# A mixture-of-experts block: the choice of experts for the second image computed in two parts, the Gelu table loaded earlier, one store on another queue

## The chip, the cores and the metric

The kernel runs on one core of a Trainium2 chip. The metric is device time in microseconds (us) of one execution, as a median over runs. The core has TensorE (matmuls, "PE" in the profile), VectorE ("DVE"), ScalarE ("ACT"), GpSimd ("POOL") and SyncE ("SP"), each working through its own list of instructions in order, with semaphores between them. SP, ACT and POOL also have a list of DMA transfers each.

## The reference, cut to what matters

Two images (batches) of 256 channels and 56 x 56 = 3136 pixels go through three stages. The first is a linear form of attention with a convolution-like mixing of channels. Its result, as 3136 tokens of 256 channels, goes through causal attention with four heads and then through a layer of eight experts, of which each token uses the two with the largest probabilities:

```python
t = _to_tokens(x)
t = t + _L1_attn_ref(_ln_t(t), L1_attn_W_attn, L1_attn_W_proj)
t = t + _L1_ffn_ref(_ln_t(t), L1_ffn_gate_w, ...)

# in _L1_ffn_ref
logits = xf @ gate_w + gate_b
probs = jax.nn.softmax(logits, axis=-1)
top2_vals, top2_idx = jax.lax.top_k(probs, 2)
cw = jnp.zeros((N, Ee)).at[jnp.arange(N)[:, None], top2_idx].add(top2_vals)
# per expert: out += cw[:, e] * (gelu(xf @ w1 + b1) @ w2 + b2)
```

All arithmetic is in 32-bit floats.

## The kernel before, in words

**Tiles.** A batch of 3136 tokens is 25 tiles of 128 rows, the last of 64 (`NCH = 25`). A tile of `ts[b]` holds the token's 256 channels, its 8 logits, and columns for mean, variance (later the inverse deviation, `RSTD`) and slot.

**Attention** (`attend`, L708 on) runs for batch 0 and then batch 1. Queries go in 7 blocks of 448 (`NB`), and for each block two pairs of heads (`hp`). One such block and pair is called a visit here. A visit goes through the key tiles up to the diagonal in steps; the last block has 25 steps a visit. A step issues the scores' matmul (L745), their Exp on ScalarE (L753), a mask on VectorE where the tile touches the diagonal (L755), the addition to the sums of exponentials on VectorE (L767), and, three steps late, the product with the values (L785). Two steps after a visit's end its sums go through a matmul (`sp`, L809), a copy, two trips through DRAM and a reciprocal; `later` holds what is due: `invert` (L829) four steps on, `scale` (L841) six after that, `hand_on`, which only counts the block as finished, two after that.

**The queue.** Everything else is written as generators, kept in `queue`. `pull(n)` gives `n` turns: it goes through the queue from the front, and the first generator that yields True has used one turn; one that yields False is passed over. Every step of attention calls `pull()` once (in `between`). So a generator nearer the front takes all turns that it can use. `tokens(b)` is the main generator of a batch: `project_out` (matmul L683, addition L688) for every tile whose block is finished, with a `closer` for its mean and variance (L177, L178, one turn a tile), and then `dispatch`.

**`dispatch(b)`** (L1028 on) begins when every tile of the batch is closed (`unclosed[b] == 0`). It is the choice of experts: an inverse square root by four Newton iterations on 128 x 25 values (L1062 to L1081), logits, softmax (Exp on ScalarE, L1098), and twice a maximum and its place (L1118 to L1130), on 128 x 25 x 8 values, up to `both`, the 0/1 table of the two chosen experts (L1136, L1139). Then come two matmuls, `rank` (L1150) and `total` (L1152), for each token's place among the tokens of its expert, the slots' arithmetic, and the distribution: each tile is normalised (L1383) and two indirect DMAs on POOL put its rows at their slots in DRAM (`x_slots`, L1391). Batch 0 does this while batch 1's attention runs, one operation per turn (`op`). Batch 1's attention is the last, so its choice runs beside the experts' work, in pieces of three to five operations per turn (`small_piece`). `one_hot` (L1254 on) makes the experts' numbers and biases of the blocks, with a matmul `bp`.

**The experts.** `experts` goes through blocks of 128 slots, one a pass (`n` from -1 on): `hidden` (matmul `ht`, L1512, then four Gelu activations, L1521), the transposes of block n + 2 (`tp`, L1489, copied by ScalarE, `xT`, L1493), the weights of a block copied by VectorE (`w`, L1500), and `outputs` of block n - 3 (`yp`, L1531, with the bias added by VectorE, L1541). Blocks up to 42 (`FULL0`) hold tokens of batch 0 alone, so these passes can run before batch 1 is chosen; the rows of blocks from 42 on are fetched in pass 36, and `need(1)` sees to it that the distribution of batch 1 is finished by then. At the end of every pass `meanwhile` counts `turn` and pulls: 4 turns while batch 1 is projected and not sent, 2 or 3 while it is being distributed, 2 otherwise.

**`closing`** is first in the queue after attention. It carries out what is left in `later` for the last visit, at set passes: `invert` after three turns, `scale` after three more, and `hand_on` in the same pass as `scale`.

**The order on each engine** is the order in which this program issues instructions (the scheduling is by hand), so a matmul from `dispatch` stands in TensorE's list behind the pass in whose `meanwhile` it was issued.

**The end.** The last columns of batch 1 are two halves of a PSUM result, copied by ScalarE and by VectorE and stored by `store_last(0)` and `store_last(1)` (L1638 to L1642), both through ScalarE's queue, with the rest of the queue's work (`settle`) between them.

Of the kernel before, what the change touches and what calls it, by code (L numbers as in the profile page):

```python
# [10 lines left out]
F32 = mybir.dt.float32  # L11
U32 = mybir.dt.uint32
I32 = mybir.dt.int32
# [15 lines left out]
def conv_attn_moe_kernel(  # L29
# [99 lines left out]
    def chunk(j):  # L129
        return min(P, N - j * P)  # L130
# [381 lines left out]
    def layer1(nm, general):  # L512

        with ExitStack() as whole:
# [361 lines left out]
            def attend_general(b, qT, kT, v):  # L876
# [5 lines left out]
                with ExitStack() as inner:  # L882
# [139 lines left out]
                    for n in range(len(order)):  # L1022
# [2 lines left out]
                        values(state)  # L1025
                        state = ahead

            def dispatch(b):  # L1028

                t = ts[b]  # L1030
                tail = chunk(NCH - 1)

                def small_piece():

# [13 lines left out]
                def small(name, last=E, dt=F32):  # L1048
                    return g1.tile([P, NCH, last], dt, tag=name, name=f"{name}_{nm}{b}")

                def wide(ap):
                    return ap.to_broadcast([P, NCH, E])

                pr = small("lg")
                red = small("red", 1)


                var = t[:, :, RSTD]
                x, y, z = (
                    small(k, 1).rearrange("p t o -> p (t o)") for k in ("newton_x", "newton_y", "red")  # L1060
                )
                nc.vector.tensor_scalar(x, var, 1e-5, None, ALU.add)  # L1062
                yield from op()
                nc.vector.tensor_scalar(
                    y.bitcast(I32), x.bitcast(I32), 1, None, ALU.arith_shift_right
                )
                yield from op()
                nc.vector.tensor_scalar(
                    y.bitcast(I32), y.bitcast(I32), -1.0, float(0x5F3759DF), ALU.mult, ALU.add
                )  # L1070
                yield from op()
                yield from small_piece()
                for i in range(4):
                    to = var if i == 3 else y
                    nc.vector.tensor_tensor(z, y, y, ALU.mult)
                    yield from op()
                    nc.vector.tensor_tensor(z, z, x, ALU.mult)
                    yield from op()
                    nc.vector.tensor_scalar(z, z, -0.5, 1.5, ALU.mult, ALU.add)
                    yield from op()  # L1080
                    nc.vector.tensor_tensor(to, y, z, ALU.mult)  # L1081
                    yield from op()
                    yield from small_piece()
                nc.vector.tensor_tensor(
                    pr, t[:, :, C : C + E], wide(t[:, :, RSTD : RSTD + 1]), ALU.mult
                )
                yield from op()
                nc.vector.tensor_tensor(
                    pr, pr, gb.unsqueeze(1).to_broadcast([P, NCH, E]), ALU.add
                )  # L1090
                yield from op()
                nc.vector.tensor_reduce(red, pr, AX.X, ALU.max)
                yield from op()
                nc.vector.tensor_tensor(pr, pr, wide(red), ALU.subtract)
                yield from op()
                yield from small_piece()
                yield from apart(3)
                nc.scalar.activation(pr, pr, AF.Exp)  # L1098
                yield from small_piece()
                yield from apart(3)  # L1100
                nc.vector.tensor_reduce(red, pr, AX.X, ALU.add)
                yield from op()
                nc.vector.reciprocal(red, red)
                yield from op()
                nc.vector.tensor_tensor(pr, pr, wide(red), ALU.mult)
                yield from op()
                yield from small_piece()


                ids = rev.unsqueeze(1).to_broadcast([P, NCH, E])  # L1110
                at = small("at")
                left = small("left")
                picks = []
                src = pr
                for k in range(2):
                    top = wts[b][:, :, k : k + 1]
                    one = small(f"one{k}")
                    nc.vector.tensor_reduce(top, src, AX.X, ALU.max)  # L1118
                    yield from op()
                    nc.vector.tensor_tensor(at, src, wide(top), ALU.is_equal)  # L1120
                    yield from op()
                    nc.vector.tensor_tensor(at, at, ids, ALU.mult)
                    yield from op()
                    yield from small_piece()
                    nc.vector.tensor_reduce(red, at, AX.X, ALU.max)
                    yield from op()
                    nc.vector.tensor_tensor(one, at, wide(red), ALU.is_equal)
                    yield from op()
                    if k == 0:
                        nc.vector.scalar_tensor_tensor(left, one, -2.0, pr, ALU.mult, ALU.add)  # L1130
                        yield from op()
                        src = left
                    picks.append(one)
                    yield from small_piece()
                both = small("both")
                nc.vector.tensor_tensor(both, picks[0], picks[1], ALU.add)  # L1136
                yield from op()
                if tail < P:
                    nc.vector.memset(both[tail:, NCH - 1], 0.0)  # L1139
                    yield from op()  # L1140
                flat = both.rearrange("p t e -> p (t e)")
                yield from small_piece()

                if b:
                    yield True
                for _ in range(0 if b else 2):
                    yield True

                rank = bank(f"rank_{b}")
# [104 lines left out]
                def one_hot(eb, w):  # L1254

                    nc.vector.tensor_copy(eblks[b], eb[:, :w])
                    hot = g1.tile([E, w], F32, tag="hot", name=f"hot_{nm}{b}")
                    nc.vector.tensor_tensor(hot, eb[:E, :w], row.to_broadcast([E, w]), ALU.is_equal)
                    yield from small_piece()
                    for _ in range(1 if b else 4):  # L1260
                        yield True
                    bp = bank(f"bp_{b}", (P, KH, w))
                    for k in range(KH):
                        nc.tensor.matmul(bp[:, k, :], b1s[:, k, :], hot, start=True, stop=True)
                    nc.vector.tensor_copy(b1bs[b], bp)
                    ranked[b] = True
                    yield from small_piece()
# [139 lines left out]
            def experts(w1s, w2s, b2s, ex, es, ps6, between, need, written, settle, decide):  # L1407
# [230 lines left out]
                def store_last(o):  # L1638

                    ot = hots[o]  # L1640
                    (nc.vector.tensor_copy if o else nc.scalar.copy)(ot, sums_of[o][:, :REST])
                    nc.scalar.dma_start(out=out[B - 1, o * P : (o + 1) * P, LAST * P :], in_=ot)  # L1642

                direct, tail, sums_of = {}, [], []

# [302 lines left out]
            if general:  # L1948
                centre_gate(bank)
                fold_gate(bank, turn_gate(bank))  # L1950
                for b in range(B):
                    xs, qks, vs = project_qkv(b, qT, kT, v, px)
                    for piece in xs(0) + [p for s in range(NS) for p in qks(s) + vs(s) + xs(s + 1)]:
                        piece()
                    attend_general(b, qT, kT, v)
                    queue.append(tokens(b, qT, lambda: N))
                    while not projected[b]:
                        pull(every=True)
            else:
# [43 lines left out]
                    piece()  # L2003
                for b in range(B):
                    batches.append(tokens(b, qT, lambda b=b: min(finished[b])))
                    queue.append(batches[b])

                    def visit(i, hp):

                        now, then = ahead(b, i, hp)  # L2010
                        ring.append(0)
                        for piece in now:
                            piece()
                        for _ in range(2):
                            products()
                        for piece in then:
                            piece()
                        ring.clear()
# [18 lines left out]
            def closing():  # L2037

                if not general:

                    while finished[B - 1][NH - 1] < N:
                        until = turn[0] + (3 if later[0][0] - clock[0] > 2 else 0)
                        while turn[0] < until:
                            yield False
                        clock[0] = max(clock[0], later[0][0])
                        due(clock[0])
# [8 lines left out]
            with ExitStack() as moe:  # L2055
# [37 lines left out]
                def meanwhile():  # L2093
                    gathered[0] = stored[0] = 0
                    turn[0] += 1
                    if placed[1] and not sent[1]:
                        pull(2 if turn[0] % 3 else 3, every=True)
                    else:
                        pull(
                            4 if worked[0] >= MIXED or projected[1] and not sent[1] else 2, every=True  # L2100
                        )
                    if side and next(side[0], None) is None:
                        side.popleft()
# [188 lines left out]
```

## Time and profile before

| | us |
|---|---|
| median of 3 runs | 1283.17 (1280.9 to 1288.38) |
| the profiled execution | 1271.12 |
| its span | 1269.3 |
| TensorE busy | 1247.0 |
| VectorE busy | 783.7 |
| ScalarE busy | 614.4 |
| GpSimd busy | 360.5 |

The span reaches from the first to the last instruction of the profiled execution. In it the convolution stage reaches to about 93 us, attention to 848, the experts from 849 to 1253, and the rest is the end. A line of the trace gives the start, the length, the engine, the source line, the operation with its output and inputs, the number of instructions and, in brackets, how long the engine stood idle before and what it was waiting for. A line of the waits gives the total, the number and the longest.

### The profile page before, as it was taken

What the parts mean: (1) busy time and instruction counts of PE and PEld (TensorE: products, weight loads), DVE (VectorE), ACT (ScalarE), POOL (GpSimd) and SP (SyncE); (2) the same over time, 40 slices, a digit from 0 to 9 for tenths busy, and PEclk for the clock granted to TensorE, in tenths of its full rate; (3) what the DMA queues carried; (4) which work ended last, traced back from release to release, by engine and by line L of the source; (5) the groups of instructions that cost most, each with busy time, mean ns of one, the idle gap of its engine ahead of it and who ended that gap; (6) DMA issues with size and microseconds to landing.
All of it is one profiled execution on the core that took longest, in us unless ns stands there. A gap on an engine that the chain in (4) does not pass through costs nothing.

```text
span 1269.3 us, 28520 instructions
## 1 busy us (share of the span) xinstructions
PE 1247.0 (98%) x10809; PEld 815.8 (64%) x10809; DVE 783.7 (62%) x1673; ACT 614.4 (48%) x1235; POOL 360.5 (28%) x319
## 2 busy tenths in 40 slices
PE   8999999999999999999999999999899999999997
PEld 8875545444444444545445444458899999999996
DVE  2583567676777754567676888764854443465563
ACT  0255555565656556455464656553333333344442
POOL 1103231110002204231111666200076212676650
PEclk9999999999999999999999999999999999999999
DMA  9995101000000000100000223542154433466653
GB/s 319 359 346 176 24 18 33 26 9 25 9 18 9 25 2 9 42 10 16 9 10 17 67 69 107 196 129 71 57 162 143 130 112 99 147 208 201 210 166 121
DMA packets 111073, 123.87 MB, mean 98 GB/s; under 512 B 19703, under 2 KB 100840, under 8 KB 110930
## 3 DMA queue, kind: packets, MB, share of 16 engines
q1 hardware_dynamic: 100130, 95.18, 24.6%
q0 software_dynamic: 9840, 25.67, 6.1%
q8 instruction: 89, 1.46, 0.5%
q10 hardware_dynamic: 960, 1.11, 0.3%
q14 instruction: 54, 0.44, 0.1%
HBM read 62.06 MB, written 61.05 MB: 97 GB/s over the span
## 4 chain that ended last, share of the span: by engine, by line
PE 95%; DVE 2%; ACT 1%; issue 0%; DMA 0%; DVEq 0%; ACTq 0%
PE yp_f L785 21%; PE sc_f L745 20%; PE ht_f L1512 14%; PE yp_f L1531 13%; PE qk_f L614 7%; PE v_f L629 4%; PE pp_f L683 3%; PE cp L410 3%; PE gram L317 2%; PE tp_f L1489 2%; PE sp_f L809 1%; PE yo_f L1758 1%; PE xp_f L600 1%; DVE acc_f L767 1%; PE tail_f L1623 0%
## 5 line engine op out<-in xcount | busy, mean ns | idle before, releaser
L767 DVE TENSOR_TENSOR acc_f<-acc_f,st_f 128x896 f32<-128x896 f32 (+5 forms) x372 | 373.0, 1003 | 127.2 <-ACT st_f L753 117.1
L753 ACT ACTIVATE st_f<-sc_f 128x896 f32<-128x896 f32 (+5 forms) x400 | 330.6, 838 | 202.4 <-PE sc_f L745 181.1
L785 PE MATMUL yp_f<-st_f,v_f 64*64 64x448 f32 (+6 forms) x3184 | 337.2, 500 | 2.7 <-DVE st_f L755 1.5
L745 PE MATMUL sc_f<-qT_f,kT_f 64*64 64x448 f32 (+6 forms) x3184 | 335.8, 498 | 1.2 <-ACT st_f L753 1.1
L1521 ACT ACTIVATE g_f<-ht_f,b1b 128x128 f32<-128x128 f32 x408 | 116.7, 369 | 218.0 <-PE ht_f L1512 217.9
L745 PEld LDWEIGHTS sc_f<-qT_f,kT_f 64*64 64x64 f32 x3184 | 119.0, 133 | 153.9 <-issue 140.4
L785 PEld LDWEIGHTS yp_f<-st_f,v_f 64*64 64x64 f32 x3184 | 116.7, 133 | 155.0 <-issue 127.5
L1512 PE MATMUL ht_f<-xT_f,w_f 128*128 128x128 f32 x1632 | 200.3, 276 | 1.4 <-ACT xT_f L1493 1.4
L1512 PEld LDWEIGHTS ht_f<-xT_f,w_f 128*128 128x128 f32 x1632 | 197.0, 192 | 6.4 <-ACT xT_f L1493 1.8
L797 POOL TENSOR_TENSOR qT_f<-acc_f 128x448 f32<-128x448 f32 x28 | 32.0, 1144 | 455.0 <-ACT acc_f L796 455.0
L1391 POOL DMA_INDIRECT x_slots<-xr_f,idx x100 | 120.7, 1207 | 140.1 <-DVE edge_f L1303 67.1
L585 POOL TENSOR_SCALAR xn_f<-t 128x256 f32<-128x256 f32 (+1 forms) x50 | 85.0, 1708 | 157.8 <-PE xp_f L600 68.6
L1500 DVE COPY w_f<-w1s_f 128x1024 f32 x102 | 72.1, 708 | 68.1 <-PE ht_f L1512 66.5
L1541 DVE TENSOR_TENSOR ys_f<-yp_f,kT_f 128x128 f32<-128x128 f32 x102 | 29.6, 290 | 102.9 <-PE yp_f L1531 102.7
L1552 POOL DMA_INDIRECT y_tokens<-ys_f,to_f x57 | 58.8, 1031 | 116.1 <-DVE ys_f L1541 94.2
L614 PE MATMUL qk_f<-px_f,wat 128*128 128x512 f32 (+2 forms) x224 | 88.2, 546 | 0.6 <-ACT px_f L606 0.6
L614 PEld LDWEIGHTS qk_f<-px_f,wat 128*128 128x128 f32 x224 | 40.6, 190 | 45.7 <-issue 41.0
L1709 POOL DMA_INDIRECT y_f<-y_slots,idx x50 | 57.2, 1144 | 17.2 <-issue 16.9
L755 DVE TENSOR_TENSOR st_f<-st_f,keep 128x256 f32<-128x256 f32 (+1 forms) x112 | 44.9, 401 | 26.9 <-ACT st_f L753 26.5
L1531 PE MATMUL yp_f<-px_f,g_f 128*128 x204 | 60.9, 380 | 0.0
L1531 PE MATMUL yp_f<-v_f,g_f 128*128 x204 | 60.7, 379 | 0.0
L1531 PE MATMUL yp_f<-kT_f,g_f 128*128 x204 | 60.7, 379 | 0.0
(285 smaller groups left out, 1224.0 us busy)
## 6 DMA issues: line engine op xcount, KB each, us to landing
x_slots<-fill SPq DMA_DIRECT2D x1, 8190.0 KB
xb_f<-x_slots SPq DMA_DIRECT2D x60, 130.0 KB
x_slots<-fill SPq DMA_DIRECT2D x1, 7296.0 KB
y_slots<-ys_f SPq DMA_DIRECT2D x57, 128.0 KB
kept<-t SPq DMA_DIRECT2D x2, 3200.0 KB
x<-in_x_dram SPq DMA_DIRECT2D x14, 448.0 KB
rb_f<-inverses SPq DMA_DIRECT2D x56, 112.0 KB
y_f<-y_tokens SPq DMA_DIRECT2D x23, 256.0 KB
```

Source lines behind the costliest of these rows:

```text
L585: nc.gpsimd.tensor_scalar(xn[:k, a], ts[b][:k, n + a, :C], ts[b][:k, n + a, MEAN : MEAN + 1], ts[b][:k, n + a, RSTD : RSTD + 1], ALU.subtr ...
L614: nc.tensor.matmul(ps[:, :w], wat[:, c, d0 : d0 + P], px[:, s % 2, c, :w], start=(c == 0), stop=(c == NH - 1),)
L745: nc.tensor.matmul(ps[h : h + HS, a, c0:W], kT[hp][rows, j * P + h : j * P + h + HS], qT[rows, hp, q0 + c0 : q0 + W], start=True, stop=True,)
L753: nc.scalar.activation(st[:k, :, c0:], ps[:k, :, c0:W], AF.Exp, scale=SCALE)
L767: nc.vector.tensor_tensor(acc[:k, :, c0:], acc[:k, :, c0:], st[:k, :, c0:], ALU.add)
L785: nc.tensor.matmul(yp[a * HS : (a + 1) * HS, h // HS, c0:W], v[hp][h : h + HS, j, a, :HS], st[h : h + HS, a, c0:], start=first, stop=bool( ...
L1391: s = nc.gpsimd.indirect_dma_start(out=xds[b], out_offset=bass.IndirectOffsetOnAxis(ap=idxs[b][:kk, k, n : n + 1], axis=0), in_=xr[:kk], i ...
L1500: nc.vector.tensor_copy(w, w1s[:, :, bass.ds(e, 1), :].rearrange("p c e h -> p c (e h)"))
L1512: nc.tensor.matmul(ht[:, k, :], w[:, c, k * P : (k + 1) * P], xT[:, c, :], start=(c == 0), stop=(c == NH - 1),)
L1521: nc.scalar.activation(g[:, k, :], ht[:, k, :], AF.Gelu, bias=b1bs[b][:, k, i : i + 1])
L1531: nc.tensor.matmul(yp[:, :C], g[:, k, :], w2s[k][:, bass.ds(e, 1), :].rearrange("p e d -> p (e d)"), start=(k == 0), stop=(k == KH - 1),)
L1552: s = nc.gpsimd.indirect_dma_start(out=y_tokens, out_offset=bass.IndirectOffsetOnAxis(ap=to[:, n % GB : n % GB + 1], axis=0), in_=ys, in_o ...
```

## The change

The choice of batch 1 is taken out of `dispatch` into `choose(b, f, e, step)`, which works on the tiles `f` to `e` and gives way after every `step` operations (for batch 1 a small operation counts half). A new generator, `choose_early`, stands in the queue ahead of batch 1's `tokens`; it starts when batch 0 is placed and 16 tiles of batch 1 are closed, and chooses for these, one operation a turn. `dispatch(1)` then chooses for the other nine. Besides:

- A Gelu activation on one element is issued in attention's last visit.
- `closing` leaves a pass between `scale` and `hand_on`.
- `bp` is issued two turns later for batch 0, one pass later for batch 1.
- During the distribution a pass gets 2 and 3 turns alternately; while the early choice isn't finished, 4.
- `store_last(1)` uses SP's queue.

```diff
+            CHOSEN = (NB - 2) * W // P // 2 * 2
+            def choose(b, f, e, step):
...
+                t = ts[b][:, f:e]
+                shape = [P, e - f, E]
+                done = [0]
+                def op(size=1):
+                    done[0] += size
+                    while done[0] >= step:
+                        done[0] -= step
                         yield True
...
+                small = 1 if b == 0 else 0.5
                 nc.vector.tensor_scalar(x, var, 1e-5, None, ALU.add)
-                yield from op()
+                yield from op(small)
...
                 nc.scalar.activation(pr, pr, AF.Exp)
-                yield from small_piece()
-                yield from apart(3)
+                for _ in range(2 if b else 3):
+                    yield True
...
+                nc.vector.tensor_tensor(both, ones_of[0], ones_of[1], ALU.add)
                 yield from op()
...
+            def choose_early(b):
+                while not placed[b - 1] or unclosed[b] > NCH - CHOSEN:
+                    yield False
+                yield from choose(b, 0, CHOSEN, 1)
+                chosen[0] = True
+            def dispatch(b):
...
+                if b:
+                    while not chosen[0]:
+                        yield False
+                    yield from choose(b, CHOSEN, NCH, 3)
+                else:
+                    yield from choose(b, 0, NCH, 1)
...
-                if b:
-                    yield True
-                for _ in range(0 if b else 2):
+                for _ in range(2):
                     yield True
                 rank = bank(f"rank_{b}")
...
-                    for _ in range(1 if b else 4):
+                    for _ in range(2 if b else 6):
                         yield True
                     bp = bank(f"bp_{b}", (P, KH, w))
...
-                    nc.scalar.dma_start(out=out[B - 1, o * P : (o + 1) * P, LAST * P :], in_=ot)
+                    (nc.sync if o else nc.scalar).dma_start(out=out[B - 1, o * P : (o + 1) * P, LAST * P :], in_=ot)
...
+                    if b:
+                        queue.append(choose_early(b))
                     queue.append(batches[b])
...
                         now, then = ahead(b, i, hp)
+                        if b + 1 == B and i + 1 == NB and hp + 1 == NH:
+                            nc.scalar.activation(warm, eps5[:1], AF.Gelu)
...
-                        until = turn[0] + (3 if later[0][0] - clock[0] > 2 else 0)
+                        until = turn[0] + (3 if later[0][0] - clock[0] > 2 else 1)
...
-                        pull(2 if turn[0] % 3 else 3, every=True)
+                        pull(2 + turn[0] % 2, every=True)
                     else:
                         pull(
-                            4 if worked[0] >= MIXED or projected[1] and not sent[1] else 2, every=True
+                            4 if worked[0] >= MIXED or projected[1] and not sent[1] or not chosen[0] else 2, every=True
                         )
```

## The prediction

> **What bounds the kernel now.** I read the page first, then who waited for whom on TensorE, TensorE in order of time around each wait, and the windows there.
>
> ```profile
> span 1269.3 us, 28520 instructions
> ...
> PE 1247.0 (98%) x10809; PEld 815.8 (64%) x10809; DVE 783.7 (62%) x1673; ACT 614.4 (48%) x1235; POOL 360.5 (28%) x319
> ```
>
> TensorE is busy all but 22.3 us of the span, so a change that removes no matmuls can win only from those 22.3 us, from a slow clock, and from what follows the last matmul. Who TensorE waited for (us in total, times, longest):
>
> ```profile
> PE rank_f L1150 <- DVE both_f L1139: 4.2, 1, 4.2
> ...
> PE ht_f L1512 <- ACT xT_f L1493: 1.4, 2, 0.8
> ...
> PE pp_f L683 <- DVE qT_f L841: 0.7, 1, 0.7
> ```
>
> All three lie where attention hands over to the experts. In order of time (start, length; idle time before it in brackets):
>
> ```profile
> 854.38 2.05 PE L1512 MATMUL ht_f<-xT_f,w_f 128*128 128x128 f32 x16 [0.61 <-ACT xT_f L1493]
> 868.96 1.60 PE L683 MATMUL pp_f<-wpr,qT_f 128*128 128x264 f32 x6 [0.67 <-DVE qT_f L841]
> 898.21 0.59 PE L1531 MATMUL yp_f<-w2s_f,g_f 128*128 x2
> 902.96 1.03 PE L1150 MATMUL rank_f<-both_f,keep 128*128 128x200 f32 x2 [4.16 <-DVE both_f L1139]
> 903.79 0.87 PE L1152 MATMUL total_f<-both_f,ones 128*128 128x200 f32 x2
> 904.46 2.73 PE L1512 MATMUL ht_f<-xT_f,w_f 128*128 128x128 f32 x16
> 907.02 0.38 PE L1489 MATMUL tp_f<-ident,xb_f 128*128 128x128 f32 x2
> ```
>
> The rank matmul stands in TensorE's order behind the experts' work of pass 12 and waits for `both`, the last result of batch 1's choice. In windows the wait is followed by a slow clock (columns: window and its length, busy us of PE, PEld, DVE, ACT and POOL with counts, then the granted clock, DMA share, GB/s):
>
> ```profile
> 902.00:904.00 2.00, 1.04 (x3) 1.04 (x4) 0.85 (x5) 0.00 (x0) 0.00 (x0) 0.67 0.19 66
> 904.00:906.00 2.00, 2.00 (x10) 2.00 (x10) 1.53 (x7) 0.00 (x0) 0.00 (x0) 0.50 0.00 0
> 906.00:908.00 2.00, 2.00 (x16) 1.92 (x16) 1.36 (x5) 0.78 (x4) 0.00 (x0) 0.98 0.00 0
> ```
>
> The whole loss there is read from spacing: a pass goes on 0.43 us after its last `yp` starts (894.48 to 894.91), and `tp` follows `ht` by 1.79. Rank and total have 200 columns where pp has 264; four pp passes take 0.89 us (874.13 to 875.02), so 4 x 0.17 = 0.68. `tp` would then be at 898.64 + 0.68 + 1.79 = 901.11; it is at 907.02. **5.9 us** are lost, 4.16 of them standing, 1.75 at a low clock.
>
> From 906 to 1240 TensorE is 20.00 of 20 us in every window: what is saved before moves the whole rest forward. The end:
>
> ```profile
> 1262.59 0.39 ACTq L1764 DMA_DIRECT2D out_dram<-ot_f  x1
> 1263.07 0.69 ACTq L1642 DMA_DIRECT2D out_dram<-hot_f  x1
> ```
>
> The last store waits its turn on ScalarE's queue, although its copy on VectorE (1261.54, 0.62 us) ended at 1262.16.
>
> **The change, part by part.**
>
> *The choice in two parts.* Before, the choice of batch 1 is 19 small operations (128x25, 0.18 us, one each 0.215) and 19 wide ones (128x200, 0.37, one each 0.40): 11.7 us of VectorE, from 884.98 on, in passes that take 3.73 us, of which weights copy and bias adds use about 1.0. VectorE can't keep pace, hence 4.16. After, passes 9 to 12 hold only nine tiles. A duration for 72 elements isn't in the trace; between 128x8 (0.16) and 128x200 (0.37) the line gives 0.155 + 1.07 ns per element, so 0.23, one each 0.26; small ones 0.20. Late part: 19 x 0.20 + 19 x 0.26 = 8.7 us. By turns: the late part counts small operations half and gives way after three units, so 6 small operations go in pass 9; 13 small and 3 wide in pass 10 (3.4 us, 0.7 over the room of 2.7); 7 wide and the wait for Exp in pass 11 (2.3); 10 wide in pass 12 (2.65). `both` is ready about 0.3 us into pass 13. The rank matmul moves one pass later, to the end of pass 13, because `hand_on` now takes a pass. It is covered by some 3 us; if VectorE were later by x, the wait returns as x - 3. Gain 5.9.
>
> Here a page speaks for less. The Trainium skill ("TensorE: Matmul & The Clock Gate", "What's actually happening") says the clock falls to half after an idle window of about 3.4 us, and that windows run freely. A gap of 4.16 then covers a full window only some of the time: by the rule the clock's 1.75 us are not lost in every run; by the row they were. I take the row, and keep 4.2 as the other end.
>
> *The early part.* It adds no work in elements, but a second set of about 39 instructions. The Trainium skill ("VectorE: DVE Perf Modes", the section on the errata) speaks against it: a fixed latency per instruction, paid by every small tile. The row says 0.155 of 0.37 us is fixed, so 38 x 0.155 = 6 us more VectorE time; on TensorE's path it would be 6 us and eat the gain. Where it lies decides. It is ready when tile 15 is closed (its statistics, L177, run at 790.86). Batch 0's distribution stands ahead of it in the queue; with two more turns before `bp` and one given away, its w1 and first row loads end three steps later, at step 8 of the last visit's 25. So the early part gets two turns before, and steps 9 to 24: 18 of its 30 turns. Its price per step: two small (0.40) or one 128x128 operation (the mask row L755 128x128: 0.28, so 0.32), beside an accumulate (1.09) in a step of 1.50: 1.49 at most, it fits. Batch 0's own choice ran one 0.36 us operation per step from 543 to 681, and TensorE lost 0.26 us between 540 and 690. The last eight steps carry masks too, and VectorE waited there 0.36, 0.39 and 0.47 us; with five operations of 0.25 to 0.32 I follow the last accumulate from 845.51 to 845.77. The sums' matmul (846.65, already waiting 0.27) moves with it: **cost 0.3**, nothing at best, 1.7 if each of the five took twice the row. Its Exp falls on step 20, before the Gelu load, so no third table switch; scores' Exps wait behind it 0.3 us on ScalarE, idle 0.6 per step.
>
> The other 12 turns go four each in passes -1, 0 and 1: 1.3 us of VectorE each between weight copies that have 2 us passes; then five closers (0.6 each) in passes 2 and 3. The weights copy of pass 2 would be about 1 us late with 3 us to spare. At nothing; if not covered up to 1.
>
> *Gelu loaded early.* ScalarE loads the table at 851.63 for 1.28 us, behind which the third block's transposed rows wait. ScalarE is idle from 845.48 to 847.30, where the load now goes. **Gain 0.6** (the bracket at 854.38); next late is nothing, as the rows would be ready at 853.05 for a start at 853.6.
>
> *hand_on a pass later.* The projection of tiles 21 and 22 no longer waits in the pass of the scaling: **gain 0.7**. It delays the choice and the distribution by one pass. The 50 indirect row stores then begin in pass 15 instead of 14, three at once, and at 2 or 3 in turn instead of 3, 2, 2: 47 left, 2.5 a pass, so through in pass 34, as needed before the fetch of pass 36. POOL takes about 1.29 us each, 3.2 of 3.73. SP's fetch behind them was at 997.95 for a use at 1005.58; not later than that.
>
> *bp two turns and one pass later:* nobody waits for it. *SP's loads three steps later:* w1 is there by 825, used at 848.
>
> *The last store on SP:* SP's queue is empty since 1256. The last issue then ends at 1262.98 instead of 1263.76: **gain 0.7**, down to 0 if the stores' transfer sets the end.
>
> Sum: 5.9 + 0.6 + 0.7 + 0.7 - 0.3 = **7.6 us**. The profiled execution took 1271.12 us (span 1269.3), so 1263.5 in its terms. The runs shown have a median of 1283.17 (1280.9 to 1288.38), 12 us above it; I know no cause for that in the trace, and take the 7.6 off the median: **1275.6 us**, 0.59%.
>
> **The rivals.**
> (A) As above, 0.68. By its own bounds (store 0 to 0.8, attention's wait 0 to 1.7) 5.5 to 8.0 us, 1275.2 to 1277.7.
> (B) In most runs the clock isn't lost, for the reason given: 7.6 - 1.75 = 5.9, 1277.3. For it: the one gap only just exceeds 3.4. Against: it did happen here. 0.15.
> (C) The wait moves: VectorE's lag at attention's end (1.7 instead of 0.3) and late weights in the opening passes (1): 5.2 us, 1278.0, and with the clock of B 1279.7. For it: the masks' steps are the fullest that VectorE has there. Against it: 3 us to spare in the opening. 0.09.
> (D) The change doesn't do it: the early part gets its turns too late and the late part is held behind it, so rank still waits; only table, projection and store are won, 1281.2. Against it: the count of turns leaves it done by pass 2, seven passes ahead. 0.04.
> (E) Slower: VectorE becomes the bound of the last visit. In 820 to 830 us it is busy 9.22 of 10. If the early part's pair of small operations cost more than 0.41 us, each of 16 steps lengthens by the excess; beyond 0.41 + 7.6/16 = 0.88 us the change loses. At 1.0 us it is 16 x 0.59 - 7.6 = 1.8 us slower, 1285. The rows' 0.18 each speak against it. 0.04.
>
> **How the numbers follow.** About 0.5% (6.4 us) is what a measurement of this kernel can tell from no change. Faster by more: most of A (0.60 of 0.68; the rest falls short), half of B and some of C (0.09 together) = 0.69. Slower: E less its near part, 0.03. Within: 0.28. The range takes A's best (1275.2) less half the runs' spread of 7.5 us, 1271.4, and a little for the unexplained 12 us, so 1270.5; on the other side C's worst and D, 1281. Beyond lie E and what the spread adds to C and D.
>
> **What would show it.** Right: no wait of rank on `both`; PEclk 1.00 from 846 to 1250; the Gelu load near 845.5; no wait of `pp` on L841; wide operations on 16 tiles between steps 16 and 24 of the last visit and just after; the last two stores on two queues. Wrong: a wait of `sp` on `acc` over 1 us, `ht` waiting for `w`, an Exp table load between 846 and 860, or a fetch after pass 36 that TensorE waits for.

## The result and the profile after

The changed kernel's median is 1279.32 us (1276.64 to 1283.66, 22 runs), the kernel before's beside it 1283.54 (1280.46 to 1289.57, 22 runs). The ratio is 0.9969, 95% interval 0.9958 to 0.9979: by the ratio 4.0 us faster (2.7 to 5.4), by the medians 4.2, where 7.6 were forecast. Gains below are differences of medians. The profiled execution took 1279.51 us.

The page of the changed kernel, and what TensorE waited for longest (total, times, longest):

```profile
span 1277.8 us, 28550 instructions
...
PE 1251.2 (98%) x10809; PEld 816.4 (64%) x10809; DVE 786.6 (62%) x1711; ACT 613.2 (48%) x1237; POOL 357.9 (28%) x319
```

```profile
PE ht_f L1541 <- issue: 6.3, 12, 1.0
PE gram L317 <- DMA xr<-in_x_rows_dram: 3.1, 1, 3.1
PE yp_f L785 <- DVE st_f L755: 2.0, 5, 0.8
PE yp_f L785 <- ACT acc_f L796: 1.8, 3, 0.6
PE yo_f L1787 <- DVE y_f L1773: 1.4, 3, 0.6
PE sc_f L745 <- ACT st_f L753: 1.4, 3, 0.6
PE yp_f L1560 <- issue: 1.3, 2, 0.8
PE ht_f L1541 <- ACT xT_f L1522: 0.8, 1, 0.8
```

The wait of `rank` on `both` (4.2) and that of `pp` (0.7) are gone, and `ht` waits for `xT` once instead of twice. New are 7.6 us of "issue" (6.3 and 1.3): TensorE pauses for which no wait is shown. The first profile of before had none.

The handover, in order of time on TensorE, its weight loads (PEld) and VectorE:

```profile
901.27 0.59 PE L1560 MATMUL yp_f<-w2s_f,g_f 128*128 x2
901.56 0.23 DVE L1128 TENSOR_TENSOR both_f<-one_f,one_f 128x72 f32<-128x72 f32 x1
901.97 0.30 PEld L1179 LDWEIGHTS rank_f<-both_f,keep 128*128 128x128 f32 x2 [0.51 <-DVE both_f L1131]
901.97 0.61 PE L1179 MATMUL rank_f<-both_f,keep 128*128 128x200 f32 x2
902.42 0.50 PE L1181 MATMUL total_f<-both_f,ones 128*128 128x200 f32 x2
902.75 1.95 PE L1541 MATMUL ht_f<-xT_f,w_f 128*128 128x128 f32 x16
```

`rank` has no bracket and runs at full clock (0.61 us, before 1.03). But its weights waited 0.51 us for `both`, and it starts at 901.97, 0.27 us after a plain pass would have gone on (901.27 + 0.43): `both` came just too late, not with 3 us to spare.

The Gelu load, in order of time, now beside the end of attention:

```profile
846.63 1.28 ACT L2045 ACT_TABLE_LOAD   x1
847.79 0.59 PE L809 MATMUL sp_f<-acc_f,ones 128*32 128x224 f32 x8 [0.27 <-DVE acc_f L767]
847.92 0.20 ACT L2045 ACTIVATE warm<-eps 1x1 f32<-1x1 f32 x1
```

The wait of `sp` on `acc` is 0.27, as before: the early part of the choice costs nothing there. The last two stores are on two queues:

```profile
1272.11 0.35 SPq L1671 DMA_DIRECT2D out_dram<-hot_f  x1
1272.51 0.38 ACTq L1793 DMA_DIRECT2D out_dram<-ot_f  x1
```

In attention, three waits of TensorE that the first profile of before doesn't have:

```profile
765.14 0.66 PE L785 MATMUL yp_f<-st_f,v_f 64*64 64x256 f32 x8 [0.44 <-DVE st_f L755]
774.67 1.73 PE L785 MATMUL yp_f<-st_f,v_f 64*64 64x448 f32 x16 [0.59 <-ACT acc_f L796]
791.76 0.98 PE L745 MATMUL sc_f<-qT_f,kT_f 64*64 64x448 f32 x8 [0.32 <-ACT st_f L753]
```

And the first of the pauses, in the matmuls of one pass:

```profile
921.41 1.28 PE L1541 MATMUL ht_f<-xT_f,w_f 128*128 128x128 f32 x10
923.35 0.27 PE L1541 MATMUL ht_f<-xT_f,w_f 128*128 128x128 f32 x1 [0.66 <-issue]
924.08 0.36 PE L1541 MATMUL ht_f<-xT_f,w_f 128*128 128x128 f32 x1 [0.46 <-issue]
924.81 0.36 PE L1541 MATMUL ht_f<-xT_f,w_f 128*128 128x128 f32 x1 [0.37 <-issue]
925.52 0.27 PE L1541 MATMUL ht_f<-xT_f,w_f 128*128 128x128 f32 x1 [0.35 <-issue]
```

One matmul starts each 0.72 us, where 16 take 1.95. In windows of the changed kernel (columns as in the prediction), TensorE stands half the time at full granted clock, while GpSimd's row stores run and the DMA share is high. Behind the pause at 1104 the clock falls as well (third line), against the forecast's "PEclk 1.00 from 846 to 1250":

```profile
922.00:924.00 2.00, 0.96 (x8) 0.69 (x6) 0.29 (x4) 0.00 (x0) 1.39 (x3) 1.00 0.85 188
924.00:926.00 2.00, 1.00 (x3) 0.48 (x3) 0.00 (x0) 0.00 (x0) 0.87 (x1) 1.00 0.73 270
...
1106.00:1108.00 2.00, 2.00 (x8) 1.73 (x8) 1.75 (x6) 2.00 (x10) 0.95 (x1) 0.50 0.60 146
```

A high DMA share beside row stores is not enough for a pause. This window is of the profile of before, where TensorE works without a gap:

```profile
926.00:928.00 2.00, 2.00 (x13) 1.79 (x12) 0.80 (x2) 1.28 (x5) 1.70 (x2) 1.00 0.76 197
```

Three points of a trace divide the span for comparison: the first `ht` of pass 0, the transposes `tp` of pass 16 (behind the handover), and the last `tp`; each column counts from the point before it. All profiles of this study, in us:

| kernel | `ht` of pass 0 at | to `tp` of pass 16 | to the last `tp` | to the end | chip |
|---|---|---|---|---|---|
| before | 849.50 | 68.71 | 325.36 | 25.7 | not named |
| before again (e0) | 850.11 | 68.88 | 333.35 | 25.7 | 7 |
| changed | 850.63 | 61.37 | 341.49 | 24.3 | not named |
| changed again (e8) | 851.01 | 61.37 | 340.33 | 24.3 | 7 |
| e1 | 849.73 | 61.36 | 340.29 | 25.4 | 7 |
| e2 | 850.51 | 63.52 | 337.08 | 25.7 | 7 |
| e3 | 852.15 | 67.95 | 339.34 | 24.3 | 7 |
| e4 | 848.72 | 61.37 | 325.36 | 25.2 | 14 |
| e5 | 849.40 | 68.68 | 325.36 | 26.1 | 14 |
| e6 | 849.36 | 62.64 | 325.36 | 25.3 | 14 |
| e7 | 849.45 | 62.64 | 325.36 | 24.4 | 14 |
| e9 | 850.77 | 61.37 | 336.71 | 24.5 | 7 |
| e10 | 849.94 | 61.36 | 335.28 | 24.3 | 10 |
| e11 | 849.75 | 61.37 | 332.89 | 24.3 | 11 |

The handover gained 68.71 - 61.37 = 7.3 us. The third stretch, which the change hardly touches, took 325.36 in the profile of before and 16.1 more in this one. The brackets of "issue" are 7.6 of the 16.1. The rest stands in rows without that name: in the matmuls between the brackets, which are drawn out (0.27 to 0.36 us each, where 16 take 1.95), in the slow clock at 1106, and in waits of `yo` on `y` (1.4).

### The profile page after: what moved, and what is told of

The parts are those of the page before. It is cut to its first block, busy times and chain, and to the rows that moved or that the text cites. A ratio compares the mean times of both kernels' runs of the same rounds, so it can differ in the third digit from the quotient of the medians.

```text
span 1277.8 us, 28550 instructions
## 1 busy us (share of the span) xinstructions
PE 1251.2 (98%) x10809; PEld 816.4 (64%) x10809; DVE 786.6 (62%) x1711; ACT 613.2 (48%) x1237; POOL 357.9 (28%) x319
## 4 chain that ended last, share of the span: by engine, by line
PE 93%; DVE 3%; issue 1%; ACT 1%; another core or an unknown queue 0%; DVEq 0%; DMA 0%; ACTq 0%
PE yp_f L785 20%; PE sc_f L745 20%; PE ht_f L1541 14%; PE yp_f L1560 13%; PE qk_f L614 7%; PE v_f L629 4%; PE pp_f L683 3%; PE cp L410 3%; PE gram L317 2%; PE tp_f L1518 2%; DVE acc_f L767 1%; PE sp_f L809 1%; PE yo_f L1787 1%; PE xp_f L600 1%; ACT st_f L753 1%
## 5 line engine op out<-in xcount | busy, mean ns | idle before, releaser
L1541 PE MATMUL ht_f<-xT_f,w_f 128*128 128x128 f32 x1632 | 203.2, 276 | 7.4 <-issue 6.3
L1560 PE MATMUL yp_f<-w2s_f,g_f 128*128 x204 | 60.7, 379 | 0.0
```

The costliest lines, as they stand in the source:

```text
L1541: nc.tensor.matmul(ht[:, k, :], w[:, c, k * P : (k + 1) * P], xT[:, c, :], start=(c == 0), stop=(c == NH - 1),)
L1560: nc.tensor.matmul(yp[:, :C], g[:, k, :], w2s[k][:, bass.ds(e, 1), :].rearrange("p e d -> p (e d)"), start=(k == 0), stop=(k == KH - 1),)
```

## The experiments

**e0: the kernel before, unchanged, once more,** to see whether the pauses are the change's.

> The kernel before, unchanged, for a second profile. The first one took 1271.12 us, 12 us less than the median of the runs, and shows no idle time of TensorE without a named wait after 906 us; the profile of the changed kernel shows about 8 us of such time between 920 and 1110 us. If those pauses come with the change, this profile has none, takes about 1271 us and has a wait of 4.2 us before rank. If they belong to most executions of either kernel, this one has about 10 us of them and takes about 1283 us; then the question is how long the wait before rank is here: 4.2 us again, or less.

Measured: 1279.72 us; runs of the same kernel beside it had a median of 1284.73 (27 runs). `rank` waited 4.18 us again, and `ht` and `tp` paused for 3.9 us (their brackets of "issue"). The third stretch is 8.0 us longer than in the first profile. So the pauses don't need the change; the first profile of before had none.

**e1: the changed kernel with `bp` of batch 0 back.**

```diff
-                    for _ in range(2 if b else 6):
+                    for _ in range(2 if b else 4):
```

> The changed kernel, with batch 0's bp where it was before (four turns, not six). In the changed kernel's profile TensorE waits 0.44, 0.59 and 0.32 us at 765, 775 and 792 us, which the first profile of before doesn't show; the steps after them are 1.1 us late. If the two turns cause that by moving batch 0's row copies into steps with a mask, these waits go and the kernel gains 1.1 us more than the change: about 5.3 us against before. If the waits come from something else, the gain stays at 4.2 us.

Measured: 1279.09 us, ratio 0.9957 (0.9941 to 0.9974) to before's 1284.73. The three waits of attention are gone; e9 and e11, which have this edit too, agree. (e1 and e9 have one wait of `sp`, 0.57 and 0.59 us, in their place; before itself has it in e0.) The four kernels with four turns start pass 0 at 849.74 on average (e1, e4, e9, e11), the four with six at 850.93 (changed, e3, e8, e10), though the two groups overlap (848.72 to 850.77, 849.94 to 852.15). So `bp`'s two turns cost some 1.2 us by these starts, 1.35 by the three waits; e8 and e10 have two such waits, of 0.9 together. The medians can't tell so little from the spread of the runs.

**e2: the kernel before with `rank` one pass later,** and nothing else but the rate of turns.

```diff
-                if b:
-                    yield True
-                for _ in range(0 if b else 2):
+                for _ in range(5 if b else 2):
                     yield True
                 rank = bank(f"rank_{b}")
...
-                        pull(2 if turn[0] % 3 else 3, every=True)
+                        pull(2 + turn[0] % 2, every=True)
```

> The kernel before with four more turns between the choice and rank, so that rank is issued one pass later, and the distribution at 2 and 3 in turn as in the change; the choice is in one piece. A pass takes 3.73 us and the wait was 4.16, so 0.4 us of waiting should be left at full clock: a gain of 5.3 us if the wait and the slow clock cost 5.9 us in most runs. If in most runs the clock isn't lost, 3.8 us. If the wait is mostly hidden in most runs, under 2 us.

Measured: 1278.78 us, ratio 0.9947 (0.9931 to 0.9963). With the choice in one piece, `rank` waits 0.45 us:

```profile
904.00 0.60 PE L1148 MATMUL rank_f<-both_f,keep 128*128 128x200 f32 x2 [0.45 <-DVE both_f L1139]
904.45 0.50 PE L1150 MATMUL total_f<-both_f,ones 128*128 128x200 f32 x2
```

The handover takes 63.52: moving the matmul in TensorE's order gives 5.2 us by itself, without the split. The rebuilt choice with its own move of `rank` gives 5.5 of the 7.3 there; the other 1.8 are the Gelu load's and `hand_on`'s.

**e3: all but the split.** The changed Gelu load, `hand_on`, `bp`, rate and store, with the choice in one piece as before.

```diff
-                        until = turn[0] + (3 if later[0][0] - clock[0] > 2 else 0)
+                        until = turn[0] + (3 if later[0][0] - clock[0] > 2 else 1)
...
+                            nc.scalar.activation(warm, eps5[:1], AF.Gelu)
```

> Every part of the change but the split: Gelu loaded early, a pass before hand_on, bp later, 2 and 3 in turn, the last store on the other queue; the choice of batch 1 is in one piece, ready as late as before, so the wait of 4.2 us before rank stays. By my sum 0.6 + 0.7 + 0.7 = 2.0 us faster than before, less 1.1 us if the two turns before bp cost that. The changed kernel's gain is 4.2, so the split itself would be worth 2.2 to 3.3 us, not 5.6. If the split is worth what I said, this one is 1.4 us slower than before.

Measured: 1281.78 us, ratio 0.9979 (0.997 to 0.9988). `rank` waits 3.77 us and the clock falls to 0.50 for 6.8 us (one window of e3; the clock is the last column but two):

```profile
907.15 1.04 PE L1150 MATMUL rank_f<-both_f,keep 128*128 128x200 f32 x2 [3.77 <-DVE both_f L1139]
...
908.00:910.00 2.00, 2.00 (x10) 2.00 (x9) 1.38 (x6) 0.00 (x0) 0.00 (x0) 0.50 0.00 1
```

Here `hand_on` is a pass later, so the choice starts a pass later as well, and `rank`, a pass later too, waits as long as before. In the change the split pays for `hand_on`'s pass; in e2, without that pass, it isn't missed. Against the changed kernel, e3 loses 67.95 - 61.37 = 6.6 us in the handover. But by the medians on chip 7 it is 3.0 us faster than before (0.9 to 2.0 were expected), where the changed kernel (e8 below) is 4.7. So of the split's 6.6 us only some 2 are left in the time, and most is taken back behind the handover.

**e4 to e7: the rate of the distribution.** The pauses begin where GpSimd has sent row stores one after another for some 8 to 10 us: 8 from 914.6 to 924.9 in the changed kernel, with the pause from 922.7 to 926. Theory one of the expectations takes these stores for the cause, theory two doesn't.

```diff
-                        pull(2 + turn[0] % 2, every=True)
+                        pull(2 + (turn[0] % 4 == 0), every=True)
```

e4 is e1 with this edit, e5 the kernel before with it (in place of its 2, 2, 3), e6 is e2 with the Gelu load and the store of the change, e7 is e6 with this edit.

> The changed kernel with bp of batch 0 back at four turns (as measured before, 5.5 us under the kernel before), and the distribution at 2, 2, 2, 3 turns a pass instead of 2, 3. Theory one: TensorE's pauses for which no wait is shown, which in that kernel add 10.2 us to the passes between 915 and 1000 us, come of row stores that GpSimd sends one after another without a gap for 10 us and more (8 stores from 913.6 to 924.0, 10 from 974.6 to 987.7); at 2.25 stores a pass of 3.73 us (2.9 us of GpSimd) no run of stores is longer than five. Then at most 3 us of pauses are left there and the time is about 7 us below, near 1272. Theory two: the pauses have nothing to do with GpSimd's stores; they stay between 8 and 11 us, and the time is that of the kernel without this edit, 12 us or more above that of theory one's ... within 2 us of 1279. Either way the pauses near 1100, where the distribution is long over, stay at 3 to 5 us.

> The kernel before with that one edit: the distribution at 2, 2, 2, 3 turns a pass instead of 2, 2, 3. Theory one: its pauses between 915 and 1000 us were 0 and 3.2 us in the two profiles; they go, so it is 0 to 3 us faster. Theory two: no difference. If the stores were late for the fetch of pass 36, a wait would stand there instead, and it would be slower by that.

> The kernel before with the rank matmul one pass later (choice in one piece, distribution at 2 and 3 turns in turn), the Gelu table loaded in attention's last visit and the last store on SP's queue; no choice in two parts, no pass for hand_on, bp as before. Without the last two edits it was 6.8 us faster than before. Each is worth its own term of the sum, 0.6 and 0.3 to 1.4: 7.7 to 8.8 us faster than before, 1276 to 1277. If the split is what the gain needs, it is no better than the changed kernel, 4 us.

> The same with the distribution at 2, 2, 2, 3 turns a pass. Theory one: the pauses of 6.8 us that the rank matmul's later place had between 915 and 1000 us fall to 3 or less, so it is 4 to 6 us faster than with 2 and 3 turns, near 1271 to 1272. Theory two: the same time as with 2 and 3 turns.

Measured, all on chip 14: before 1271.58 us (1270.43 to 1272.42, 17 runs), e4 1262.22 (0.993, 0.9916 to 0.9943), e5 1271.52 (0.9999, 0.9991 to 1.0007), e6 1264.14 (0.9943, 0.993 to 0.9957), e7 1263.83 (0.9941, 0.9927 to 0.9954). None of these four profiles has a pause, e6 with 22 stores in a row from 915.2 to 946.2 included. The third stretch is 325.36 in all four. e6 is 7.4 us faster than before, a little under the 7.7 to 8.8 expected. The rate was not tested here: there are no pauses, and the kernel before runs as in its first profile (1271.12). Neither theory is hit; both had left out that the pauses go with the chip. Without pauses the rate is worth nothing (e5), and the changed kernel without `bp`'s shift is 9.4 us faster than before. e4 is 1.6 us under e7, of which the handover has 62.64 - 61.37 = 1.3: `hand_on`'s pass (0.94, below) and what the split adds. What e4's TensorE still waits for, the start of the waits view:

```profile
PE gram L317 <- DMA xr<-in_x_rows_dram: 3.1, 1, 3.1
PE yp_f L785 <- DVE st_f L755: 1.5, 4, 0.8
PE yp_f L785 <- ACT acc_f L796: 1.2, 2, 0.6
```

**e8 and e9: the changed kernel and e4 once more, side by side.**

> The changed kernel as it is, once more. The profiles fall into two sorts: with TensorE's pauses, in which the kernel before has a median near 1284 us, and without any, in which it is at 1271.6. Theory one: the pauses belong to the chip that runs it, and the change is worth its sum where there are none. If this chip has none, the changed kernel is 1.1 us (the three attention waits that bp's two turns bring) above the 1262.2 of the version with bp back at four turns and the slower distribution, so 1263.3, 8.2 us under the kernel before; the prediction's sum says 7.6. If this chip has them, it is 3 to 5 us under, as measured first. Theory two: the change itself makes pauses that the kernel before does not have, by 2.5 stores a pass instead of 2.33. Then pauses of 4 us or more stand in its profile between 915 and 1000 us on a chip where the kernel before is near 1271.6, and it is again only 4 us faster.

> The changed kernel with bp back at four turns and the distribution at 2, 2, 2, 3 turns, once more, on the chip of the run beside it. On a chip without pauses: 9.4 us under the kernel before, and 1.1 us under the changed kernel, all of it bp's. On a chip with pauses: if they come of GpSimd's stores in close order, it is 7 us or more under the changed kernel; if not, 1 to 2 us, which is bp's part.

Measured, on chip 7: before 1283.24 us (26 runs), changed 1278.57 (0.9959, 0.9946 to 0.9973; 4.7 us by the medians), e9 1278.74 (0.9968, 0.9954 to 0.9981). The changed kernel's first result repeats. e9 is no faster, against theory one. Its trace says why the edit is a weak test: turns are not stores, and with fewer turns there are still 8 stores in a row from 914.7 to 925.0, and a pause from 923.

**e10: the changed kernel with the stores themselves limited.**

```diff
                     for k in range(2):
+                        while b and paced[0] >= (3 if turn[0] > 31 else 2):
+                            yield False
+                        paced[0] += 1
...
                     turn[0] += 1
+                    paced[0] = 0
```

> The changed kernel with one limit added: in the distribution no pass sends more than two rows' stores, up to about pass 30, and no more than three after it (in the changed kernel two and three in turn, and up to four in the first pass). GpSimd then works 2.6 of 3.73 us, with a gap in every pass, up to about 970 us, and almost without a gap from there to the end of the distribution. On a chip where the kernel before is near 1284: by theory one (the pauses come of stores in close order) the pauses between 915 and 970 us, which were 5.7 us in the changed kernel's last profile, go, those after 970 stay or grow, and it is 3 to 6 us faster than the changed kernel's 1278.6. By theory two (the pauses need no such row of stores) TensorE still pauses near 925, by 3 us or more, and the time is within 2 us of 1278.6. On a chip where the kernel before is near 1271.6 there are no pauses to remove: then the run tells what the change is worth without them, 8 us under the kernel before (1263.3) if only bp's 1.1 us separates it from the 9.4 measured with bp back, and 4 if the change itself makes pauses.

Measured, on a third chip (10): 1274.8 us against before's 1281.46, ratio 0.9947 (0.9931 to 0.9964), 6.7 us faster. Up to 970 the stores come in fours with a gap behind each, and TensorE doesn't pause; every pass from 911 to 988 takes exactly what it takes in the profiles without pauses. Then 12 stores follow each other from 983.4 to 998.7, and TensorE pauses 10 us into them. GpSimd and TensorE in order of time:

```profile
944.54 0.98 POOL L1424 DMA_INDIRECT x_slots<-xr_f,idx  x1 [0.30 <-issue]
945.83 0.98 POOL L1424 DMA_INDIRECT x_slots<-xr_f,idx  x1 [0.30 <-issue]
949.44 0.97 POOL L1424 DMA_INDIRECT x_slots<-xr_f,idx  x1 [2.63 <-DVE xr_f L1419]
...
992.62 1.05 POOL L1424 DMA_INDIRECT x_slots<-xr_f,idx  x1 [0.30 <-issue]
994.11 0.38 PE L1564 MATMUL yp_f<-kT_f,g_f 128*128 x1 [0.91 <-issue]
996.24 0.59 PE L1564 MATMUL yp_f<-w2s_f,g_f 128*128 x2 [0.51 <-issue]
999.79 0.60 PE L1545 MATMUL ht_f<-xT_f,w_f 128*128 128x128 f32 x2 [1.63 <-issue]
```

That is theory one's picture in one trace: the same code pauses where the stores are close and not where they aren't. It is one trace, and it doesn't show that the stores are the cause. The changed kernel was not run on chip 10, so how much of the 6.7 us is the limit's isn't known. The pauses near 1100 stand, behind nine indirect transfers from 1089.1 to 1101.1.

**e11: that limit to the end, and `bp` back.** The limit is `2 if turn[0] % 4 else 3`.

> The changed kernel with bp of batch 0 back at four turns and no more than two stores a pass in the distribution, three in every fourth, to its end. With at most two stores a pass up to pass 30 it was 6.7 us faster than before; left in that profile were 6.5 us of pauses behind twelve stores in a row (983.4 to 998.7) and the 1.1 us of bp. By theory one (close order) no more than five stores stand in a row before the last ones, so some 4 of the 6.5 go, and bp's 1.1: 11 to 12 us faster than before on a chip where that is near 1283. By theory two the pauses come back near 925 and it is 6 to 8 us faster. On a chip where the kernel before is near 1271.6 there is nothing to win from the limit: 9.4 us faster, as measured there with bp back.

Measured, on a chip without pauses (11): 1271.32 us, before 1271.49, ratio 1.0001 (0.9993 to 1.0009). None of the expected numbers. The limit made the distribution late: the last stores ended at 1001.4, SP issued the fetch of pass 36 behind them at 1003.08, and TensorE waited for the fetched rows, with a slow clock behind:

```profile
1001.61 1.95 PE L1545 MATMUL ht_f<-xT_f,w_f 128*128 128x128 f32 x16
1009.39 0.66 PE L1522 MATMUL tp_f<-ident,xb_f 128*128 128x128 f32 x2 [5.83 <-DVE xb_f L1499]
```

The two passes there take 6.0 and 1.55 us over their length. So the limit cost 7.5 us here, and what it does against pauses e11 can't tell. A version that wins on both sorts of chip was not found: e4 is the best measured without pauses (9.4 us), e10 with them (6.7; e2 had 6.0).

## Why the prediction was right and wrong

**The wait of `rank` and the slow clock, 5.9: right in cause, 0.4 too high.** The passes around `rank` take 6.59 us over a plain pass before and 1.06 after: 5.5. Of the 1.06, 0.27 are `rank`'s late start and 0.78 `rank` and `total` themselves (901.97 to 902.75), where I had worked out 0.68. Rival B has nothing for it: the clock was lost in all three profiles of before (6.59, 6.75, 6.56 us over a plain pass), at 0.50 for 3.41 us, and in e3 behind a wait of 3.77. From the free-running window of the Trainium skill ("TensorE: Matmul & The Clock Gate", "What's actually happening") the prediction took that a gap of 4.16 us would cost the clock only some of the time. It was right to set that behind the row: gaps of 4.16, 4.18 and 4.18 us all cost it.

**"`both` is ready about 0.3 us into pass 13 ... covered by some 3 us": wrong.** It was ready at 901.92, 3.9 us into the pass that began at 897.97. The turns fell as counted, but work issued at the end of a pass runs beside the next one: the ten operations given to pass 12 ran from 899.16 to 901.79. The forecast had the cover wrong by more than 3 us and was saved by its size, which was used up to the last 0.27 us. That `rank`'s place alone nearly does it, e2 shows.

**Gelu 0.6 and `hand_on` 0.7: right, a little low.** From the start of pass 0 to `tp` of pass 4 the changed kernel takes 0.87 less (11.64 for 12.51), and from there to pass 12 0.94 less. e6, with the Gelu load and without the split, has the same 11.64; e3, with `hand_on`'s pass and without the split, the same 0.94. With the 5.5 that makes the 7.3 of the table.

**The early part, 0.3: nothing.** `sp` waits 0.27 before and after.

**"`bp` two turns and one pass later: nobody waits for it": wrong, some 1.2 us.** Nobody waits for `bp`, but the two turns push what stands behind it in the queue, batch 0's distribution, into other steps of attention. That these turns are the cause, e1 shows, where the three waits are gone; that it is VectorE's masks which they meet is read from `st` and `acc` in the brackets alone, and not shown. I followed the shift into the steps of the early part, and not into those before.

**The last store, 0.7: right, a little low.** From the last `tp` to the end it is 25.8 on average in the four profiles with the old queue and 24.6 in the ten with the new: 1.15 less, from 0.3 to 1.7 by the single profiles. Why e1, e4 and e6 gain least (25.2 to 25.4) isn't known.

**"I know no cause for that in the trace, and take the 7.6 off the median": the step that failed.** The measured 1279.3 us lies inside the stated range, but 3.7 us above the forecast, and this step is where most of those were lost. The profile shown is of an execution without pauses; the median shown with it (1283.17, against 1271.12) is like those measured where there are pauses. The 12 us aren't a constant. Without pauses the terms measured here sum to 7.3 + 1.15 - 1.2 = 7.25 us, an estimate for the changed kernel, which itself was run on no such chip; e4, without the 1.2 loss, measured 9.4 there, 8.6 to 8.8 in its span. With pauses the changed kernel's third stretch is 15.0 and 16.1 us longer (e8 and the first profile, both near their medians), while the kernel before loses some 12 to 13 (8.0 in e0, an execution 5.0 under its median; 1283.24 - 1271.5 by medians). So some 3 of the 7.25 us went into more pauses, and 4.2 and 4.7 were measured. That even the 7.25 is so near to the 7.6 is in part luck: the 0.4 too much at `rank` and the 1.2 at `bp` are nearly made good by some 0.5 too little at Gelu and `hand_on`, 0.45 at the store and 0.3 at the early part.

Why the changed kernel pauses more isn't settled. e1, with the split, has 14.9, e2 and e3, without it, 11.7 and 14.0, at the same rate of turns. But e3's profile is of the slowest of its 22 runs, 3.7 us above their median. If each third stretch is moved by the distance of its profile from its kernel's median (an estimate), the three with the split at this rate have 14.8 to 15.9 (changed, e8, e1), those without it some 12 and 10.3 (e2, e3). So what pauses more seems to go with the split; by which way isn't shown. The instruction fetches don't tell the two cases apart either: between 880 and 1150 us those of queue q8, of 16 KB each, take 0.9 to 2.4 us in the profiles with pauses and 0.9 to 2.1 in those without.

Of the other rivals, D and E left no trace, and of C only the tightness of `both`. The distribution was through in time for pass 36, as counted.

## What to carry to other kernels

When a matmul stands in order behind a result that is late, first ask what it costs to issue it later: moving `rank` by one pass gave 5.2 us by itself, where the rebuilt choice gave 5.5. When a profile is 1% under the median of the runs beside it, a sum made in it holds for that execution only; find out what the difference is made of before it is carried over as a constant. And in a queue that shares out turns, one delay moves everything behind it, so each neighbour's new place has to be checked.

## What the runs showed of the hardware

**Pauses.** On some chips (7 and 10) TensorE pauses with no wait shown, one matmul each 0.72 us at full granted clock, mostly 8 to 12 us into an unbroken series of indirect DMAs from GpSimd. Not every such series has a pause: in e8 those from 928.5 to 939.1 and from 962.6 to 973.6 have none. On others (14 and 11) there are no pauses, with up to 26 such DMAs in a row. Chip 7 ran twice, half an hour apart, with pauses both times, the others once each. That it is the chip, and not something else that differed between these times, is likely but not shown. With stores in fours the pauses were absent in the one trace that has this. What TensorE lacks in a pause the trace doesn't show.

**The clock.** In the experts' part it fell to 0.50 in every wait of 3.77 to 5.83 us (before, e0, e5, e3, e11), for 3.41 or 6.83 us, and not in the wait of 0.45 us (e2). Behind some pauses it fell too, for 3.41 us (changed kernel at 1106, e8 at 927, e10 at 999), although TensorE was not idle all through them: in the changed kernel it was busy 1.01 of the 2 us from 1102 and 0.81 of those from 1104.

**Spread.** The runs of one kernel spread over 1.3 to 3.4 us on chips without pauses, over 3.2 to 9.1 on the others.
